# One softmax shift per unit, added as the exponential's bias, in an attention kernel with an FP8 feed-forward

## The chip, the core and the metric

The kernel runs on one core of a Trainium2 chip. A core has five engines that run their own in-order instruction streams: TensorE (PE in the profile, with its weight loads listed apart as PEld), VectorE (DVE), ScalarE (ACT), GpSimd (POOL) and SyncE (SP). DMA transfers are issued by some of these and run beside them. The metric is the device time of one execution in microseconds (us); less is better. Before the change the median of three runs is 1726.01 us (1724.27 to 1728.25).

## The reference

The input x has 2 batches of 2048 rows of 512 values. What has to be computed, cut to its core:

```python
x = x + attention(layernorm(x))              # 16 heads of 32, 2 groups of keys and values
x = x + ffn(layernorm(x))                    # one 512x512 product, both sides rounded to FP8

q, k = rope(xn @ wq + bq) * 32**-0.5, rope(xn @ wk + bk)
scores = q @ k_of_the_group.T * 32**-0.5     # 2048 x 2048 for each head
attn   = softmax(scores)                     # exp(s - m) / sum(exp(s - m)), for any shift m of a row
out    = (attn @ v) @ wo + bo
```

A softmax needs no particular shift: any number m that is the same for a whole row cancels between the exponentials and their sum. The shift only keeps the exponentials in the range of the number format.

## The kernel before, in words

**Units, rounds and chunks.** Attention is done in 64 units. A unit `u` is one block of 512 queries, four heads ("quad") and one half of the block: 4 heads x 256 queries against all 2048 keys. The keys are taken in 16 chunks of 128, four to a round, so a unit has four rounds, `r` = 0 to 3. A chunk's scores stand transposed in PSUM, keys on the 128 partitions and 4 x 256 queries along the row: tile `T`, in one of two buffers, even chunks in one and odd chunks in the other.

**A chunk.** `probabilities` (L1008) has PE multiply the stacked keys `dkS` with the stacked queries `qst` (two matmuls of 512 columns, L1022), and ACT takes the exponential of the 128x1024 scores into `p` (L1031). The score matmuls of chunk c+2 wait until the exponential of chunk c has read the buffer. Keys are stored as differences against the key 256 places earlier, so that chunk c+2 adds to what stands in the buffer (`start=False`); the scores of chunks 0 and 1 open each buffer.

**The shift before.** For each unit the maximum of every row's scores over the first 128 keys is found a unit ahead. `first_scores` (L511) runs in rounds 0 and 1 of the unit before: four matmuls (L523) and a DVE maximum per head and query (L531). `split_maxima` (L500) splits the maxima into two addends in round 2 (L504, L505). `gather_maxima` (L538) transposes them on PE in round 3 (L543) and ACT copies them to `mT` (L547). When the unit starts, four matmuls (L1013) with the constant matrix `sel`, which holds -1, write the negated maxima of all queries into each of the two buffers ahead of the scores. The exponential's bias is a constant.

**Values and sums.** One round later, `weigh` multiplies the `p` of the round with the values (L968, 16 products, `avs`), and the sums of the exponentials are gathered: DVE adds `p` of chunks 0 and 1 to `pair` and of chunks 2 and 3 to a second tile (`add_pair`, L1005); a DMA that GpSimd issues adds `pair` onto the second (`accumulate`, L1035), which leaves one tile `far[r]` a round. DVE joins some of these (`join`, L1038), and PE multiplies what is left with a matrix of ones (`sum_up`, L986), which sums over the partitions. `in_two` says for which units (all but the last three) two tiles are left. Then `keep_values` (L1056) and `finish_heads` (from L935) divide: ACT copies the sums and takes Ln and Exp (L942, L943), DVE does three products (L946 to L948). `seen` collects the sums, so that the end of the program can tell whether some sum was out of range; if so, a slow general version in the same program runs.

**The order of the work.** It is written out by hand: within `manual_schedule` every engine executes its instructions in the order in which the code issues them. In a round the code issues: scores and exponentials of the first two chunks, their sum on DVE, the value products of the round before, `sum_up` of the unit before where due, up to two DVE pieces of other work (`fill(ON_DVE, 2)`), in round 3 a join and `gather_maxima`; then the scores and exponentials of the last two chunks, their sum, `first_scores` in rounds 0 and 1, one or two PE pieces of other work (`fill(ON_PE, ...)`; a piece is one chunk of a projection, two recorded matmuls of 512 columns), and again up to two DVE pieces. The other work is a queue of jobs: projections of queries and keys for later blocks, the output projection, the second layer norm. The job `finish_heads` comes ahead of these.

**Buffers.** `first_scores` and `gather_maxima` use the PSUM bank `s0`, one at a time; the other work uses `s1`. The tiles `far` have four buffers, those of `pair` three, `p` seven.

Of the kernel before, what the change touches and what calls it, by code (L numbers as in the profile page):

```python
# [8 lines left out]
F32 = mybir.dt.float32  # L9
F32R = mybir.dt.float32r  # L10
BF16 = mybir.dt.bfloat16
U32 = mybir.dt.uint32
AF = mybir.ActivationFunctionType
ALU = mybir.AluOpType
AX = mybir.AxisListType

P = 128
HEADS = 16
GROUPS = 2
HD = 32  # L20
TB = 512
NT = TB // P
EPS = 1e-5
E4M3_MAX = 448.0
# [3 lines left out]
def preln_attn_fp8_ffn_kernel(  # L28
# [37 lines left out]
    nc = tc.nc  # L66
# [19 lines left out]
    AV_BANKS = 2  # L86
    FIRST = P
    MOST_BITS = float(0x5D5E0B6B)

    const = ctx.enter_context(tc.tile_pool(name="const", bufs=1))  # L90
    xpool = ctx.enter_context(tc.tile_pool(name="x", bufs=3))
# [90 lines left out]
    ones = const.tile([P, HD], F32, tag="ones", name="ones")  # L182
    nc.gpsimd.memset(ones, 1.0)

    sel = const.tile([P, 4, P], F32R, tag="sel", name="sel")
    nc.gpsimd.memset(sel.bitcast(F32), 0.0)
    for j in range(4):
        nc.gpsimd.memset(sel[j * HD : j * HD + 2, j, :].bitcast(F32), -1.0)
    mrow = const.tile([P, HB], F32R, tag="mrow", name="mrow")
    nc.gpsimd.memset(mrow.bitcast(F32), 0.0)  # L190


    def layernorm_stats(src, mean, rstd, name, tiles=range(NT)):
# [17 lines left out]
    def quantized_scale(amax, scale, inv, name):  # L211

        across = bank(f"across_{name}")
        nc.tensor.transpose(across[:1, :P], amax, ident)
        whole = small.tile([1, 1], F32, tag="whole", name=f"whole_{name}")
        nc.vector.tensor_reduce(whole, across[:1, :P], AX.X, ALU.max)
        give_back()
        down = bank(f"down_{name}")

        nc.tensor.matmul(down[:, :1], sel[:1, 0, :].bitcast(F32), whole, start=True, stop=True)  # L220
        nc.vector.tensor_scalar(scale, down[:, :1], -1.0 / E4M3_MAX, 1e-12, ALU.mult, ALU.max)
        give_back()
        nc.vector.reciprocal(inv, scale)

# [269 lines left out]
    def group(k):  # L494
        return quads[k][1] // (QUADS // GROUPS)

    split = []
    largest = {}

    def split_maxima():  # L500

        if split:
            mview, mx = split.pop()
            nc.vector.tensor_copy(mview[:, :, :, 0], mx)  # L504
            nc.vector.tensor_tensor(  # L505
                mview[:, :, :, 1], mx, mview[:, :, :, 0].bitcast(F32), ALU.subtract
            )

    def first_scores(u, i):

        k, half = units[u]
        if i == 0:
            largest[u] = small.tile([P, HT, 4], F32, tag="mx", name=f"mx_{u}")
        mx = largest[u]
        s = ps_s.tile([P, 4, FIRST], F32, tag="s0", name=f"s_{u}_{i}")  # L520
        at = (half * HT + i) * P
        for j in range(4):
            nc.tensor.matmul(  # L523
                s[:, j, :],
                qst[k][:, j, at : at + P],
                stacked["dkS"][:, group(k), :FIRST],
                start=True,
                stop=True,
                skip_group_check=True,
            )  # L530
        nc.vector.tensor_reduce(mx[:, i, :], s, AX.X, ALU.max)  # L531
        if i == HT - 1:
            mview = mrow.rearrange("p (i j r) -> p i j r", i=HT, j=4)
            split.append((mview, largest.pop(u)))

    maxima = {}

    def gather_maxima(u):  # L538

        split_maxima()  # L540
        tp = ps_s.tile([P, TB], F32, tag="s0", name=f"mtp_{u}")
        for i in range(HT):
            nc.tensor.transpose(  # L543
                tp[:, i * P : (i + 1) * P], mrow[:, i * P : (i + 1) * P].bitcast(F32), ident
            )
        mT = wide.tile([P, HB], F32R, tag="mT", name=f"mT_{u}")
        nc.scalar.copy(mT, tp[:, :HB])  # L547
        maxima[u] = mT


    mean2 = const.tile([P, NBLK, NT], F32, tag="mean2", name="mean2")
# [150 lines left out]
    with tc.manual_schedule():  # L702
        xnT = {
            0: wide_block("xnT", "xnT_kv_0"),
            1: wide_block("attn", "xnT_kv_1", 2),
            2: wide_block("attn", "xnT_kv_2", 2),
            3: wide_block("qst", "xnT_kv_3", 2),
        }
        kv = {n: project_kv(n, x_kv[n], xnT[n], tables[n]) for n in (0, 1)}
        q0 = project_q(0, xnT[0], tables[0])  # L710
        run(first(kv[0], FRONT))
        together((kv[0], 1), (first(kv[1], FRONT), 2))
        x_kv[3] = load_x(3, "kv")
        kv[2] = project_kv(2, x_kv[2], xnT[2], load_tables(2))
        w_all = ppool.tile([P, DC, D], BF16, tag="p", name="w_ffn")
        nc.sync.dma_start(w_all, w_ffn.rearrange("(c p) k -> p c k", p=P))
        queries = first(q0, 1 + QUERIES)
        together((kv[1], 1), (queries, 1), (first(kv[2], FRONT), 2))
        assert (0, 0) in q_far
        stack_queries(0)  # L720
        nc.sync.dma_start(wo_sb, wo.rearrange("(c p) n -> p c n", p=P))
        queries = first(q0, QUERIES)
        together((kv[2], 1), (queries, 1))
        kv[3] = project_kv(3, x_kv[3], xnT[3], load_tables(3))

        run(first(kv[3], FRONT))
        run(prepare_weight(w_all))
        for i in range(HT):
            first_scores(0, i)
        run(first(kv[3], MIDDLE))  # L730
        gather_maxima(0)
        run(kv[3])


# [71 lines left out]
        return 2 if r >= 2 and owed > (ROUNDS + r - 2) * left else 1  # L806

    seen = const.tile([P, len(units)], F32, tag="seen", name="seen")
    without_x = {}
    x_res = {}  # L810
    x_taken, x_done = [], set()
# [122 lines left out]
    def finish_heads(u, both, sums):  # L934
# [4 lines left out]
        nc.scalar.activation(total, sums, AF.Copy, accum_out=seen[:, u : u + 1])  # L939
        yield LATER  # L940
        yield ON_DVE
        nc.scalar.activation(guess, total, AF.Ln)  # L942
        nc.scalar.activation(guess, guess, AF.Exp, scale=-1.0)  # L943
        yield LATER
# [30 lines left out]
                    skip_group_check=True,  # L975
                )

    def in_two(u):

        return 0 <= u < len(units) - 3  # L980

# [26 lines left out]
    def probabilities(u, T, kc):  # L1008

        k, half = units[u]  # L1010
        if kc < 2:
            for j in range(4):
                nc.tensor.matmul(  # L1013
                    T[:, j, :],
                    sel[:, j, :],
                    maxima[u],
                    start=(j % 2 == 0),
                    stop=True,
                    skip_group_check=True,
                )  # L1020
        for j in range(0, 4, 2):
            nc.tensor.matmul(  # L1022
                T[:, j : j + 2, :],
                stacked["dkS"][:, group(k), kc * P : (kc + 1) * P],
                qst[k][:, j : j + 2, half * HB : (half + 1) * HB],
                start=False,
                stop=True,
                skip_group_check=True,
            )
        p = ppool.tile([P, 4, HB], F32, tag="p", name=f"p_{u}_{kc}")  # L1030
        nc.scalar.activation(p, T, AF.Exp, scale=SCALE)  # L1031
        return p

    def accumulate(to, of):
# [2 lines left out]
    def join(to, of):  # L1037
        nc.vector.tensor_tensor(to, to, of, ALU.add)  # L1038
# [19 lines left out]
    with tc.manual_schedule():  # L1058
        behind = None
        before = None  # L1060
        for u, (k, half) in enumerate(units):
# [13 lines left out]
            for r in range(ROUNDS):  # L1075
# [13 lines left out]
                if behind:  # L1089
                    weigh(*behind)  # L1090
                if before and r == 0:
                    parts = before.far[1 : 2 if in_two(before.u) else 3]
                    sum_up(before.avs[:, 1, :], parts, False, False)
                    keep_values(before)
                elif before and r == (2 if in_two(before.u) else 1):
                    sum_up(before.avs[:, 1, :], before.far[3:], False, True)
                    finishing.append(
                        Job(finish_heads(before.u, before.both, before.avs[:, 1, :]))
                    )
                fill(ON_DVE, 2)  # L1100
                if r == 2:
                    split_maxima()
                if last:
                    join(unit.far[1], unit.far[0])
                    if u + 1 < len(units):
                        gather_maxima(u + 1)

                probs.append(probabilities(u, banks[0], chunks[2]))
                probs.append(probabilities(u, banks[1], chunks[3]))
# [1 line left out]
                    unit.far.append(add_pair(u, chunks[2], *probs[2:]))  # L1111
                    accumulate(unit.far[r], pair)
                add_some_bias()
                if before and r == 1 and in_two(before.u):
                    join(before.far[3], before.far[2])
                behind = unit, chunks, probs
                if r < HT and u + 1 < len(units):
                    first_scores(u + 1, r)
                fill(ON_PE, pieces(u, r, ending_soon))
                fill(ON_DVE, 2)  # L1120
            before = unit
# [77 lines left out]
            multiplied(n, i, ready)  # L1199
            ready = ahead  # L1200

    top = small.tile([P, 1], F32, tag="top", name="top")
    nc.vector.tensor_reduce(top, seen.bitcast(U32), AX.X, ALU.max)
    across = bank("across_seen")
    nc.tensor.transpose(across[:1, :P], top, ident)
    flag = small.tile([1, 1], mybir.dt.int32, tag="flag", name="flag")
    nc.vector.tensor_reduce(top[:1], across[:1, :P], AX.X, ALU.max)
    nc.vector.tensor_scalar(flag, top[:1], MOST_BITS, None, ALU.is_gt)
    over = nc.values_load(flag, min_val=0, max_val=1)


# [259 lines left out]
```

## Time and profile before

| what | value |
|---|---|
| median of three runs | 1726.01 us |
| the profiled execution | 1724.88 us, span 1723.0 us |
| granted TensorE clock, mean over the span | 0.975 |
| PE / DVE / ACT / POOL busy | 1575.1 / 1248.8 / 1236.4 / 317.1 us |
| exponentials, L1031 | 1024 of 1024 ns, 992.6 us busy |
| scores, L1022 | 2048 matmuls, 680.0 us busy |
| value products, L968 | 8192 matmuls, 495.1 us busy |
| shift matmuls, L1013 | 512 matmuls, 94.5 us busy |
| sum products, L986 | 1048 matmuls, 80.7 us busy |
| the units run | from 99 to 1608 us of the span |

A line of a group names the kernel's line, the engine, the operation, the tile written and the tiles read, the shapes, the number of instructions, then "busy us, mean ns of one", and at last the time in which the engine stood idle just before them with what ended it. A matmul in float32 is recorded as two instructions. Matmuls overlap each other, so the sum of their lengths is more than the busy time. A line of a timeline begins with the start and the length in us and merges neighbours of a kind. "PEclk" is the share of its full clock that TensorE was granted. The chain is followed back from the last instruction, at each step to what released it.

### The profile page before, as it was taken

Reading aid. Unit: us, or ns where it says so; the run is one execution under the profiler, and the core shown is the slowest. Engines: PE = TensorE matmul, PEld = TensorE weight load, DVE = VectorE, ACT = ScalarE, POOL = GpSimd, SP = SyncE. Lnnn points to the kernel's source line nnn. Section 1 sums busy time; section 2 is a strip of 40 time slices with the busy share of each in tenths; the row PEclk is TensorE's granted clock in tenths of the full one; section 3 lists DMA queues with packets and bytes.
Section 4 is the critical chain, followed back from the end, with each engine's and each line's share of the span. In section 5 each row is a group of like instructions: output and inputs, shape, how many; then the busy total and the mean of one; then the engine's idle time right before and its main releaser. Section 6 shows DMA issues by size and latency. Waiting matters only on the chain.

```text
span 1723.0 us, 33241 instructions
## 1 busy us (share of the span) xinstructions
PE 1575.1 (91%) x13483; PEld 900.6 (52%) x13483; DVE 1248.8 (72%) x1673; ACT 1236.4 (72%) x1629; POOL 317.1 (18%) x381
## 2 busy tenths in 40 slices
PE   5499999999999999999999999999999989999565
PEld 2255555555555555555555555555555555555222
DVE  4447677677887769776877687767777686676697
ACT  2257877777777777777777777877777777777375
POOL 3321112211212112211221122111211122111100
PEclk9699999999999999999999999999999999999888
DMA  6657769867778767878786688656867597576222
GB/s 203 201 122 178 170 146 216 195 127 160 184 178 164 183 153 160 192 147 195 175 196 134 118 199 177 152 117 154 184 149 154 105 203 145 116 187 138 56 86 112
DMA packets 105810, 272.61 MB, mean 158 GB/s; under 512 B 15920, under 2 KB 16560, under 8 KB 102960
## 3 DMA queue, kind: packets, MB, share of 16 engines
q0 software_dynamic: 41328, 142.10, 44.2%
q1 hardware_dynamic: 61904, 126.92, 25.3%
q8 instruction: 108, 1.77, 0.4%
q10 hardware_dynamic: 2416, 1.38, 0.3%
q14 instruction: 54, 0.44, 0.1%
HBM read 87.36 MB, written 40.89 MB: 74 GB/s over the span
## 4 chain that ended last, share of the span: by engine, by line
PE 67%; DVE 10%; DMA 8%; issue 7%; ACT 5%; SPq 2%; POOL 1%; ACTq 0%; DVEq 0%; POOLq 0%
PE avs L968 23%; PE T L1022 23%; PE po L295 5%; ACT p L1031 5%; PE pq L295 4%; PE T L1013 3%; PE avs L986 3%; PE s L523 2%; DMA pa<-pa 2%; DMA qst<-q_far 2%; PE pk L295 2%; PE mtp L543 1%; DVE v L236 1%; DVE pa L1005 1%; DMA sw_q<-q 1%
## 5 line engine op out<-in xcount | busy, mean ns | idle before, releaser
L1031 ACT ACTIVATE p<-T 128x1024 f32<-128x1024 f32 x1024 | 992.6, 1024 | 178.3 <-PE T L1022 171.1
L1005 DVE TENSOR_TENSOR pa<-p,p 128x1024 f32<-128x1024 f32 x511 | 624.7, 1223 | 356.1 <-ACT p L1031 355.0
L1022 PE MATMUL T<-qst,dkS 128*128 128x512 f32 x2048 | 680.0, 442 | 24.8 <-ACT p L1031 23.8
L968 PE MATMUL avs<-p,vX 128*32 128x256 f32 x8192 | 495.1, 382 | 0.0
L1022 PEld LDWEIGHTS T<-qst,dkS 128*128 128x128 f32 x2048 | 338.7, 188 | 273.6 <-ACT p L1031 153.5
L1035 POOL DMA_DIRECT2D pa<-pa x255 | 221.0, 867 | 1201.2 <-DVE pa L1005 915.3
L968 PEld LDWEIGHTS avs<-p,vX 128*32 128x32 f32 x8192 | 239.9, 109 | 225.8 <-issue 93.9
L1038 DVE TENSOR_TENSOR pa<-pa,pa 128x1024 f32<-128x1024 f32 x125 | 152.3, 1219 | 16.0 <-DMA pa<-pa 15.9
L295 PE MATMUL po<-wo_sb,attn 128*128 128x512 f32 x256 | 129.6, 603 | 0.0
L295 PE MATMUL pq<-xnT_q,wq_sb 128*128 128x512 f32 x224 | 111.8, 601 | 0.0
L1013 PE MATMUL T<-mT,sel 128*128 128x256 f32 x512 | 94.5, 307 | 6.5 <-ACT p L1031 6.1
L1013 PEld LDWEIGHTS T<-mT,sel 128*128 128x128 f32 x512 | 72.9, 188 | 46.9 <-ACT p L1031 30.8
L986 PE MATMUL avs<-pa,ones 128*32 128x256 f32 x1048 | 80.7, 382 | 11.9 <-DVE pa L1038 11.1
L531 DVE TENSOR_REDUCE mx<-s 128x4 f32<-128x512 f32 x128 | 87.5, 683 | 2.8 <-PE s L523 2.8
L1056 ACT COPY both<-avs 128x256 f32<-128x256 f32 x64 | 23.9, 373 | 86.7 <-PE avs L986 86.7
L523 PEld LDWEIGHTS s<-dkS,qst 128*128 128x128 f32 x512 | 77.2, 192 | 14.7 <-DVE mx L531 3.1
L939 ACT ACTIVATE both<-avs 128x256 f32<-128x256 f32 x64 | 24.6, 385 | 71.7 <-PE avs L986 71.7
L523 PE MATMUL s<-dkS,qst 128*128 128x128 f32 x512 | 72.8, 265 | 2.2 <-DVE mx L531 2.1
L295 PEld LDWEIGHTS po<-wo_sb,attn 128*128 128x128 f32 x256 | 44.3, 190 | 17.6 <-issue 11.0
L986 PEld LDWEIGHTS avs<-pa,ones 128*32 128x32 f32 x1048 | 27.8, 109 | 43.7 <-DVE pa L1038 30.4
L295 PEld LDWEIGHTS pq<-xnT_q,wq_sb 128*128 128x128 f32 x224 | 39.4, 190 | 17.4 <-issue 13.5
L1171 PE MATMUL xtp<-ident_bf,xq 128*128 128x128 bf16 x128 | 16.0, 266 | 34.3 <-DVE xq L237 34.3
(128 smaller groups left out, 1033.0 us busy)
## 6 DMA issues: line engine op xcount, KB each, us to landing
pa<-pa POOLq DMA_DIRECT2D x255, 512.0 KB, 5.2
qst<-q_far SPq DMA_DIRECT2D x128, 256.0 KB, 7.0
q_far<-hi_q SPq DMA_DIRECT2D x32, 256.0 KB, 4.6
q_far<-lo_q SPq DMA_DIRECT2D x32, 256.0 KB, 4.5
x_res<-in_L_attn_x_dram SPq DMA_DIRECT2D x16, 512.0 KB, 10.8
x_res<-in_L_attn_bo_dram POOLq DMA_DIRECT2D x32, 256.0 KB, 6.7
out_dram<-v SPq DMA_DIRECT2D x16, 512.0 KB, 2.8
sw_q<-q SPq DMA_DIRECT2D x240, 32.0 KB, 3.1
```

What stands on the lines that cost most here:

```text
L295: nc.tensor.matmul(dst, lhs(c), rhs(c), start=(c == 0), stop=(c == chunks - 1))
L523: nc.tensor.matmul(s[:, j, :], qst[k][:, j, at : at + P], stacked["dkS"][:, group(k), :FIRST], start=True, stop=True, skip_group_check=True,)
L531: nc.vector.tensor_reduce(mx[:, i, :], s, AX.X, ALU.max)
L939: nc.scalar.activation(total, sums, AF.Copy, accum_out=seen[:, u : u + 1])
L968: nc.tensor.matmul(av[j * HD : (j + 1) * HD, :], vX[batch(k)][:, kc, group(k), :], p[:, j, :], start=(kc == 0), stop=(kc == NTS - 1), tile ...
L986: nc.tensor.matmul(dst[j * HD : (j + 1) * HD, :], ones, part[:, j, :], start=start and i == 0, stop=stop and i == len(parts) - 1, tile_pos ...
L1005: nc.vector.tensor_tensor(pa, a, b, ALU.add)
L1013: nc.tensor.matmul(T[:, j, :], sel[:, j, :], maxima[u], start=(j % 2 == 0), stop=True, skip_group_check=True,)
L1022: nc.tensor.matmul(T[:, j : j + 2, :], stacked["dkS"][:, group(k), kc * P : (kc + 1) * P], qst[k][:, j : j + 2, half * HB : (half + 1) * H ...
L1031: nc.scalar.activation(p, T, AF.Exp, scale=SCALE)
L1035: nc.gpsimd.dma_start(out=to, in_=of, accum_op=ALU.add)
L1038: nc.vector.tensor_tensor(to, to, of, ALU.add)
```

## The change

Each unit now has a single shift instead of one for every row. The maximum of the scores over the first 128 keys is taken over all heads and queries of the unit, multiplied by -1/32 and handed to the exponential as its bias, a column of 128 equal numbers.

- `first_scores` is one matmul of 512 columns in each of rounds 0 and 1, with keys on the partitions, and a DVE maximum over the row.
- `gather_largest`, at the end of round 2 behind the sum of chunks 2 and 3 and ahead of the PE pieces: DVE takes the larger of the two columns in bf16, PE transposes that column to one row, DVE takes its maximum.
- `spread_largest`, in round 3 behind the sum products: PE multiplies the number with a row of -1/32 in bf16, so that it stands on 128 partitions. `make_shift`, behind the join of round 3: DVE copies it to SBUF.
- The eight matmuls with `sel` at a unit's start are gone, the scores of chunks 0 and 1 open the buffers, and the exponential takes `shift` as bias.
- For all units but the last three, DVE joins `far[1]` and `far[2]` to `far[3]` in rounds 1 and 2 of the next unit, and there is one sum product, in round 3 instead of rounds 0 and 2. The job `finish_heads` starts one round later.
- `finish_heads` also takes the least sum of each unit, and the end of the program tests it too.

```diff
+    scales = const.tile([1, P], BF16, tag="scales", name="scales")
+    nc.gpsimd.memset(scales, -SCALE)
...
     def first_scores(u, i):
...
-        for j in range(4):
-            nc.tensor.matmul(
-                s[:, j, :],
-                qst[k][:, j, at : at + P],
-                stacked["dkS"][:, group(k), :FIRST],
...
-        nc.vector.tensor_reduce(mx[:, i, :], s, AX.X, ALU.max)
...
+        s = ps_s.tile([FIRST, 2, HB], F32, tag="s0", name=f"s_{u}_{i}")
+        nc.tensor.matmul(
+            s,
+            stacked["dkS"][:, group(k), :FIRST],
+            qst[k][:, 2 * i : 2 * i + 2, half * HB : (half + 1) * HB],
...
+        nc.vector.tensor_reduce(
+            largest[u][:, i : i + 1], s.rearrange("p j t -> p (j t)"), AX.X, ALU.max
+        )
+
+    def gather_largest(u):
+
+        mx = largest.pop(u)
+        top = small.tile([P, 1], BF16, tag="top_u", name=f"top_{u}")
+        nc.vector.tensor_tensor(top, mx[:, :1], mx[:, 1:], ALU.max)
+        across = ps_s.tile([P, TB * 2], BF16, tag="s0", name=f"across_{u}")
+        nc.tensor.transpose(across[:1, :P], top, ident_bf)
+        largest[u] = small.tile([1, 1], BF16, tag="whole_u", name=f"whole_{u}")
+        nc.vector.tensor_reduce(largest[u], across[:1, :P], AX.X, ALU.max)
+
+    def spread_largest(u):
+
+        down = ps_s.tile([P, TB], F32, tag="s0", name=f"down_{u}")
+        nc.tensor.matmul(down[:, :1], scales, largest.pop(u), start=True, stop=True)
+        shift[u] = down
+
+    def make_shift(u):
+
+        down = shift[u]
+        shift[u] = small.tile([P, 1], F32, tag="shift_u", name=f"shift_{u}")
+        nc.vector.tensor_copy(shift[u], down[:, :1])
...
         nc.scalar.activation(total, sums, AF.Copy, accum_out=seen[:, u : u + 1])
         yield LATER
         yield ON_DVE
+        nc.vector.tensor_reduce(least[:, u : u + 1], total, AX.X, ALU.min)
         nc.scalar.activation(guess, total, AF.Ln)
...
     def probabilities(u, T, kc):
...
-        if kc < 2:
-            for j in range(4):
-                nc.tensor.matmul(
-                    T[:, j, :],
-                    sel[:, j, :],
-                    maxima[u],
...
-                start=False,
+                start=kc < 2,
...
-        nc.scalar.activation(p, T, AF.Exp, scale=SCALE)
+        nc.scalar.activation(p, T, AF.Exp, bias=shift[u], scale=SCALE)
...
                 if before and r == 0:
-                    parts = before.far[1 : 2 if in_two(before.u) else 3]
-                    sum_up(before.avs[:, 1, :], parts, False, False)
+                    if not in_one(before.u):
+                        sum_up(before.avs[:, 1, :], before.far[1:3], False, False)
                     keep_values(before)
-                elif before and r == (2 if in_two(before.u) else 1):
+                elif before and r == (3 if in_one(before.u) else 1):
                     sum_up(before.avs[:, 1, :], before.far[3:], False, True)
...
+                if last and u + 1 < len(units):
+                    spread_largest(u + 1)
                 fill(ON_DVE, 2)
-                if r == 2:
-                    split_maxima()
                 if last:
                     join(unit.far[1], unit.far[0])
-                    if u + 1 < len(units):
-                        gather_maxima(u + 1)
+                elif before and r > 0 and in_one(before.u):
+                    join(before.far[3], before.far[r])
+                if last and u + 1 < len(units):
+                    make_shift(u + 1)
...
                 add_some_bias()
-                if before and r == 1 and in_two(before.u):
-                    join(before.far[3], before.far[2])
                 behind = unit, chunks, probs
-                if r < HT and u + 1 < len(units):
+                if r < 2 and u + 1 < len(units):
                     first_scores(u + 1, r)
+                if r == 2 and u + 1 < len(units):
+                    gather_largest(u + 1)
                 fill(ON_PE, pieces(u, r, ending_soon))
                 fill(ON_DVE, 2)
```

Ahead of the first unit the same calls take the place of `first_scores` and `gather_maxima`. At the end of the program DVE reduces `seen` and `least`, tests both against their bounds and takes the larger verdict, instead of reducing and testing `seen` alone.

## The prediction

> **What bounds the kernel now.** I read the page's shares first, then its chain, the groups, one unit in the timeline, and last the clock.
>
> ```profile
> span 1723.0 us, 33241 instructions
> PE 1575.1 (91%) x13483; PEld 900.6 (52%) x13483; DVE 1248.8 (72%) x1673; ACT 1236.4 (72%) x1629; POOL 317.1 (18%) x381
> PE 67%; DVE 10%; DMA 8%; issue 7%; ACT 5%; SPq 2%; POOL 1%; ACTq 0%; DVEq 0%; POOLq 0%
> L1013 PE MATMUL T<-mT,sel 128*128 128x256 f32 x512 | 94.5, 307 | 6.5 <-ACT p L1031 6.1
> L986 PE MATMUL avs<-pa,ones 128*32 128x256 f32 x1048 | 80.7, 382 | 11.9 <-DVE pa L1038 11.1
> ```
>
> PE is busy 91% of the time and holds 67% of the chain. The last two lines are most of what the change takes from PE: 94.5 us and half of 80.7 us. If PE were the only limit, that would be a gain of some 130 us. So I ask of each round whether PE really ends it. Here are rounds 2 and 3 of one unit, first PE, then ACT and DVE (start, length):
>
> ```profile
> 965.43 1.62 PE L1022 MATMUL T<-qst,dkS 128*128 128x512 f32 x4
> 966.98 1.93 PE L968 MATMUL avs<-p,vX 128*32 128x256 f32 x32
> 968.73 0.62 PE L986 MATMUL avs<-pa,ones 128*32 128x256 f32 x8
> 969.28 1.19 PE L1022 MATMUL T<-qst,dkS 128*128 128x512 f32 x4
> 970.31 1.02 PE L295 MATMUL po<-wo_sb,attn 128*128 128x512 f32 x2
> 971.18 0.73 PE L1022 MATMUL T<-qst,dkS 128*128 128x512 f32 x2
> 972.10 0.73 PE L1022 MATMUL T<-qst,dkS 128*128 128x512 f32 x2 [0.18 <-ACT p L1031]
> ...
> 970.10 3.85 ACT L1031 ACTIVATE p<-T 128x1024 f32<-128x1024 f32 x4 [0.21 <-PE T L1022]
> ...
> 972.08 1.23 DVE L1005 TENSOR_TENSOR pa<-p,p 128x1024 f32<-128x1024 f32 x1 [1.40 <-ACT p L1031]
> ```
>
> Call a round's four chunks c0 to c3. PE issues c2 and c3 at 969.28, their exponentials run from 970.10, the second ends at 972.05, and only then do two things start: DVE's sum of both (972.08), and PE's scores for c1 of the next round (972.10), which need c3's bank. So a round is a loop of PE and ACT. Cutting the same timeline finer gives its links: from c1's first score matmul to c2's second one 2.81 us, from there to c2's exponential 0.49, two exponentials 1.94 (they start 0.92 apart and the last takes 1.02), and 0.06 to the next c1: 5.30 us, which is round 1 (961.02 to 966.32). One piece of projection (0.86 us) fits beside ACT; with two pieces (1.72) PE ends the loop instead. Units with one piece per round last 22.8 us, those with two in rounds 2 and 3 last 23.9.
>
> **The change part by part.** I follow c1's first score matmul from round to round, in the one-piece unit: before, 5.66 (r=0), 5.30 (r=1), 5.78 (r=2), 6.07 (r=3).
>
> *Exponential with a bias tile.* The bias was a constant, now it is a column in SBUF. The nearest rows have the same size, with and without such a column:
>
> ```profile
> L439 ACT ACTIVATE q<-pq,bq_sb 128x512 f32<-128x512 f32 x32 | 22.1, 689 | 3.7 <-PE pq L295 3.7
> L285 ACT COPY xnT_kv<-tp_kv 128x512 f32<-128x512 f32 x32 | 18.9, 590 | 20.8 <-PE tp_kv L282 20.8
> ```
>
> That is 99 ns more each; the start of the next instruction comes 0.10 later too (585 against 482 ns), so overlap doesn't hide it. I take 0.095 us for each of 1024 exponentials. In the loop a pair costs 2.13 instead of 1.94. Ends: 0 (hidden) to 0.10.
>
> *Shift matmuls (L1013), 8 a unit.* Four stood ahead of c0 and four ahead of c1 in round 0, 0.12 us apart, 0.95 in all. In a one-piece unit the first four lie in PE's wait for c3's bank; the other 0.48 are saved. With two pieces all 0.95 are.
>
> *First scores.* 4 matmuls (0.41 us) become one of 512 columns (0.23), in rounds 0 and 1. Both lie between c3's scores and the wait for c3's exponential: worth nothing, because ACT ends that stretch. If that cover went, 0.18 twice.
>
> *Sum products.* Two groups of 0.54 us become one, moved to r=3. They stand between c1 and c2, on the loop: r=0 and r=2 save 0.54 each, r=3 pays 0.54.
>
> *Transposes and the copy mT.* Two transposes at r=3 (0.37 us) go; the matmul that spreads the maximum comes in the same place. Its nearest row, the spread of a scale at L220, takes 0.24 alone; I take 0.2, ends 0.05 and 0.36. The copy (0.27 of ACT) was in ACT's wait for c2, so nothing.
>
> *The new transpose at r=2: the decisive item.* It stands on PE right behind c3's scores, ahead of the projection piece and the whole next round. It needs the maximum over two columns, which DVE does behind its sum of c2 and c3 in its in-order queue; that sum waits for c3's exponential. In the unit shown: c3's exponential would end at 972.05+0.19 = 972.24, the sum starts 0.03 later, the next instruction on DVE 1.14 after that (so follow the sums), 973.41; a small one takes 0.17, 973.58; a release of PE by DVE takes 0.07 (L1038's end at 968.66 to 968.73); loading one column 0.08 (L214). The transpose runs at 973.73 and the piece follows at 973.85 instead of 970.31: 3.54 later. Then 0.86 and 0.46 (c0) to c1 at 975.17 instead of 972.10, 3.07 later, less 0.49 because the sums no longer delay c2: +2.6. PE had had its last score matmul at 970.08, 0.40 long, so it idles 3.2 us. A transpose itself lies between 0.05 and 0.37 (L214), taken at 0.12.
>
> *DVE.* Per unit: third join +1.14, least value +0.35 (half of the 128x512 reduction's 0.68), two halves of the old split -0.35, three small ones +0.5: +1.7 on about 17.7 of 23.6 us. Between the sums of c2 and c3 in rounds 1 and 2 it then does two sums 2.3, one join 1.14, one reduction 0.6: 4.0 of 5.5 us, leaving 1.5 for filler. I take no delay; the cover goes where two or more fillers of 0.6 come. The reduction of one row waits about 0.4 for the transpose with only filler behind it; the copy of the shift waits for the spread with the sum of c2 and c3 behind it, which isn't ready by then. The exponential that uses the shift is 6 us later. The joins moved past nothing on SP or POOL; no DMA is added.
>
> *The heads' end, one round later.* Ln and Exp move on ACT from r=3 to r=0, where the value copy is. From 958.35 before; without the sums it would start at about 0.2 ahead of c2's second score matmul (2.6 after c1), then 0.27, 0.45 and 0.35: c2's exponential can start at 3.7, not 3.3. So r=0 becomes 3.7+2.13+0.06 = 5.89 (before 5.66): +0.23, although PE lost 1.2 us of work there.
>
> *Sum of a unit.* r=0 +0.23; r=1 5.49, +0.19; r=2 +2.6; r=3: 2.81+0.54+0.2+0.49+2.13+0.06 = 6.23, +0.16: +3.2. With two pieces: +0.23, +0.19, +3.1 (the second piece is no longer hidden in ACT's wait), and r=3 PE-bound 6.42 for 6.76, -0.34: again +3.2. Of the 64 units 63 have the new transpose: +202. PE's waits for joins ahead of the sums (11.9 us in the row above) mostly go: -10. Before and behind the units a few small instructions, +1.5.
>
> *The clock.* Does a 3.2 us hole cost TensorE its clock? The clock in the records changes on a grid of 3.41 us. Windows of that grid (length, PE busy, clock):
>
> ```profile
> core 0: us, PE busy (x), PEclk, DMA share, GB/s
> 1647.18:1650.59 3.41, 1.60 (x11) 1.00 0.21 82
> 1650.59:1654.00 3.41, 1.26 (x9) 1.00 0.41 156
> 1654.00:1657.41 3.41, 2.78 (x13) 0.50 0.21 80
> ```
>
> After 1.81 us idle in a window the clock stays; after 2.15 it is 0.50 for the whole next one. Another window with 1.90 idle (1616.46) lost it too. So the limit is near 1.85. A hole of 3.2 us, put anywhere on the grid, leaves 1.85 in one window in about 87% of positions. The next window then has 2.8 to 3.4 us of PE work at half speed: matmuls of 0.43 took 0.85 in such a window (90.70). If only scores and projections slow, 1.0 us a unit on average; if the value products do too, 1.3. I take 1.16 x 63 = 73; ends 0 and 85.
>
> The Trainium skill weighs this otherwise. Its page "TensorE: Matmul & The Clock Gate" (section "Why this matters for your kernels") asks for no idle gap over about 3 us and names one whole window of idle as the condition; by its 3.4 us window this hole would just keep the clock, and the sum would be 1918. The trace's 1.90 and 2.15 us decide for me.
>
> The profiled execution took 1724.88 us (1723.0 span and 1.9 around it), 1.1 below the median of 1726.01, which is nothing here. 1724.9 + 202 - 10 + 1.5 + 73 = 1991.
>
> **The rivals.**
> - *The clock holds.* For it: in the stretch of the units the clock never fell, even with a hole of 2.4 us; against it: that hole was split over two windows, 1.00 and 1.43. Then 1918.
> - *DVE becomes late.* One filler more ahead of the maximum in every unit: 0.6 x 63 = +38, 2029; two, 2067. For it: 1.5 us of slack only; against it: 0.68 to 1.9 us of idle before most of its sums.
> - *Not slower: the maximum is there in time.* If the transpose found it ready, r=2 would be 5.49 for 5.78, and a one-piece unit would come out even (+0.23+0.19-0.29+0.16 = +0.3, less the waits); a two-piece one -0.2. About 1715, and 1675 if the bias column were free as well. It decides only if PE waits less than about 0.25 us a unit, where I work out 3.2; the order of the two DVE instructions in the code is against it.
>
> **How the numbers follow.** Stall and clock 0.52, the clock holds 0.25, DVE late 0.14, in time 0.04; 0.05 for a stall half covered by something not seen. The range goes from below the second case (1918 with a free bias column, 0.76 x 35 one-piece units = -27) to the third: 1890 to 2060. Differences below 0.2% (3.5 us) can't be told from none: faster 0.04, same 0.02, slower 0.94.
>
> **What would show it.** PE idle 3.2 us before the new transpose, released by DVE's small maximum, 63 times; exponentials of 1.12 us; L1005 and then the maximum at c3's end in round 2; half-clock windows right behind, the granted clock of the run falling from 0.975 to about 0.92; units of 27 us. I am wrong if the transpose comes without a wait, or if the exponentials stay at 1.02.

## The result and the profile after

The changed kernel takes 2059.99 us, median of four runs (2055.94 to 2060.61), against 1726.38 before. The ratio is 1.193 (95% interval 1.191 to 1.195): 19% slower, 334 us. The forecast was 1991 with a range of 1890 to 2060, so the sign and the main reason hold. That the time lies inside the range at all is luck: it is 0.01 us from the edge, and two of the four runs are beyond it. The 69 us more than forecast need a cause of their own.

The page of the changed kernel, its shares, chain, and the groups that answer to those of before, with the new transpose:

```profile
span 2057.9 us, 30646 instructions
PE 1624.0 (79%) x12094; PEld 836.6 (41%) x12099; DVE 1351.9 (66%) x1865; ACT 1291.2 (63%) x1565; POOL 315.6 (15%) x377
PE 38%; DVE 28%; ACT 15%; issue 8%; DMA 5%; SPq 3%; POOL 1%; ACTq 0%; DVEq 0%; POOLq 0%
L1018 ACT ACTIVATE p<-T,shift 128x1024 f32<-128x1024 f32 x1024 | 1070.9, 1112 | 446.2 <-PE T L1009 432.6
L527 PE MATMUL across<-ident_bf,top 128*1 128x128 bf16 x64 | 15.8, 247 | 252.1 <-DVE top L525 252.1
```

PE went from 91% to 79% busy, and no engine took its place: DVE and ACT are less busy in share too. The chain says why: PE's part fell from 67% to 38%, DVE's rose from 10% to 28% and ACT's from 5% to 15%. The engines now wait for each other in turn. The last line names the place: PE stood idle for 252.1 us ahead of 64 small transposes, released by DVE's small maximum `top`; the matmuls themselves take 15.8 us. That is 4.00 us for each of the 63 waits. Exponentials take 1112 ns for 1024.

One unit in the timeline of the changed kernel, round 2 and the start of round 3; PE, then ACT and DVE:

```profile
1199.38 1.21 PE L1009 MATMUL T<-qst,dkS 128*128 128x512 f32 x4
1203.73 0.22 PE L527 MATMUL across<-ident_bf,top 128*1 128x128 bf16 x1 [3.13 <-DVE top L525]
1203.87 1.77 PE L294 MATMUL po<-wo_sb,attn 128*128 128x512 f32 x2
1204.65 2.70 PE L1009 MATMUL T<-qst,dkS 128*128 128x512 f32 x4
...
1200.22 2.12 ACT L1018 ACTIVATE p<-T,shift 128x1024 f32<-128x1024 f32 x2 [1.41 <-PE T L1009]
...
1202.37 1.22 DVE L1002 TENSOR_TENSOR pa<-p,p 128x1024 f32<-128x1024 f32 x1 [0.60 <-ACT p L1018]
1203.52 0.15 DVE L525 TENSOR_TENSOR top<-mx 128x1 bf16<-128x1 f32 x1
```

Read it from 1200.22: two exponentials end at 1202.34, DVE's sum starts 0.03 later, `top` follows at 1203.52, the transpose at 1203.73. PE had been idle for 3.13 us by then. The projection behind the transpose takes 1.77 us where it took 1.02 before, and four score matmuls 2.70 instead of 1.20, because of the clock. The two windows of the clock's grid (length, PE busy, clock) that hold this stretch:

```profile
core 0: us, PE busy (x), PEclk, DMA share, GB/s
1200.81:1204.22 3.41, 0.50 (x2) 1.00 0.52 98
1204.22:1207.64 3.41, 3.41 (x10) 0.50 0.52 101
```

With 2.91 us idle in the first, the second ran at half speed. In the stretch of the units the records hold 300 us at half clock, 88 windows of 3.41; before there were none. The granted clock of the whole run fell from 0.975 to 0.906.

### The profile page after: what moved, and what is told of

Its sections match the earlier page's. It is cut to its first block, busy times and chain, and to the rows that moved or that the text cites. A ratio compares the mean times of both kernels' runs of the same rounds, so it can differ in the third digit from the quotient of the medians.

```text
span 2057.9 us, 30646 instructions
## 1 busy us (share of the span) xinstructions
PE 1624.0 (79%) x12094; PEld 836.6 (41%) x12099; DVE 1351.9 (66%) x1865; ACT 1291.2 (63%) x1565; POOL 315.6 (15%) x377
## 4 chain that ended last, share of the span: by engine, by line
PE 38%; DVE 28%; ACT 15%; issue 8%; DMA 5%; SPq 3%; POOL 1%; ACTq 0%; DVEq 0%; POOLq 0%
PE avs L965 14%; PE T L1009 12%; ACT p L1018 12%; DVE pa L1002 11%; DVE pa L1025 5%; PE po L294 4%; PE pq L294 4%; DMA pa<-pa 3%; SPq L307 2%; DVE mx L517 2%; PE avs L983 1%; PE pk L294 1%; DVE v L235 1%; DMA qst<-q_far 1%; ACT both L940 1%
## 5 line engine op out<-in xcount | busy, mean ns | idle before, releaser
L1018 ACT ACTIVATE p<-T,shift 128x1024 f32<-128x1024 f32 x1024 | 1070.9, 1112 | 446.2 <-PE T L1009 432.6
L1009 PE MATMUL T<-qst,dkS 128*128 128x512 f32 x2048 | 736.8, 471 | 77.7 <-ACT p L1018 75.3
L1009 PEld LDWEIGHTS T<-qst,dkS 128*128 128x128 f32 x2048 | 367.6, 201 | 425.9 <-ACT p L1018 275.3
L965 PE MATMUL avs<-p,vX 128*32 128x256 f32 x8192 | 519.9, 396 | 0.0
L1025 DVE TENSOR_TENSOR pa<-pa,pa 128x1024 f32<-128x1024 f32 x186 | 226.3, 1216 | 9.2 <-DMA pa<-pa 9.2
L527 PE MATMUL across<-ident_bf,top 128*1 128x128 bf16 x64 | 15.8, 247 | 252.1 <-DVE top L525 252.1
L294 PE MATMUL pq<-xnT_q,wq_sb 128*128 128x512 f32 x224 | 135.3, 713 | 0.0
L517 DVE TENSOR_REDUCE mx<-s 128x1 f32<-128x512 f32 x128 | 87.4, 683 | 2.1 <-PE s L510 2.1
L510 PE MATMUL s<-qst,dkS 128*128 128x512 f32 x128 | 51.8, 405 | 0.8 <-DVE mx L517 0.8
L281 PE MATMUL tp_kv<-ident,xn_kv 128*128 128x128 f32 x128 | 23.6, 328 | 27.2 <-DVE xn_kv L262 26.6
L294 PE MATMUL pk<-xnT_kv,wkv_sb 128*128 128x512 f32 x64 | 39.3, 727 | 7.4 <-ACT xnT_kv L284 7.4
```

Source lines behind the costliest of these rows:

```text
L281: nc.tensor.transpose(tp[:, c * P : (c + 1) * P], xn[h][:, c * P : (c + 1) * P], ident)
L294: nc.tensor.matmul(dst, lhs(c), rhs(c), start=(c == 0), stop=(c == chunks - 1))
L510: nc.tensor.matmul(s, stacked["dkS"][:, group(k), :FIRST], qst[k][:, 2 * i : 2 * i + 2, half * HB : (half + 1) * HB], start=True, stop=True,)
L517: nc.vector.tensor_reduce(largest[u][:, i : i + 1], s.rearrange("p j t -> p (j t)"), AX.X, ALU.max)
L965: nc.tensor.matmul(av[j * HD : (j + 1) * HD, :], vX[batch(k)][:, kc, group(k), :], p[:, j, :], start=(kc == 0), stop=(kc == NTS - 1), tile ...
L1009: nc.tensor.matmul(T[:, j : j + 2, :], stacked["dkS"][:, group(k), kc * P : (kc + 1) * P], qst[k][:, j : j + 2, half * HB : (half + 1) * H ...
```

## The experiments

Every kernel was timed beside the kernel before on the same chip; ratios are to that. "After" is the changed kernel.

### The place of the stall, its clock, DVE's lateness and the bias column

**top_early**: DVE takes the larger column a round earlier, so that the transpose finds it ready.

```diff
+    def larger_column(u):
+
+        mx = largest.pop(u)
+        largest[u] = small.tile([P, 1], BF16, tag="top_u", name=f"top_{u}")
+        nc.vector.tensor_tensor(largest[u], mx[:, :1], mx[:, 1:], ALU.max)
+
     def gather_largest(u):
 
-        mx = largest.pop(u)
-        top = small.tile([P, 1], BF16, tag="top_u", name=f"top_{u}")
-        nc.vector.tensor_tensor(top, mx[:, :1], mx[:, 1:], ALU.max)
+        top = largest.pop(u)
...
                     first_scores(u + 1, r)
+                if r == 1 and u + 1 < len(units):
+                    larger_column(u + 1)
```

> One edit to the changed kernel: DVE takes the larger of the two columns at the end of round 1, right behind the maximum of the second first scores, instead of at the end of round 2 behind the sum of chunks 2 and 3; the transpose on PE stays where it is. Theory 'stall' (PE waits at the transpose because DVE reaches the maximum only behind that sum): the wait of 252 us before the transpose goes, the clock stays at 1.00 through the units, and the time is what the bias column and the heads' end leave of the savings, 1690 to 1730 us. Rival 'ACT' (the loss is the longer exponentials and the later Ln and Exp on ACT, and the wait at the transpose only shows time that ACT would take anyway): over 1900 us. In between, 1740 to 1890: both.

Measured: 1776.02 us, ratio 1.029 (1.025 to 1.032). One small instruction moved in DVE's queue gives back 284 of the 334 us. The wait before the transpose falls from 252 us to 15.6. So the stall at that place is shown, and the rival "ACT" (over 1900) is out. But the time is above the 1690 to 1730 that the theory asked for. One-piece units come out as worked out in the prediction's third rival, nearly even: 22.92 us against 22.81. The 50 us that are left sit in 19 units, which are over 1 us longer than before. Here is the end of one such unit, DVE and then ACT of top_early:

```profile
764.90 0.75 DVE L312 SCALAR_TENSOR_TENSOR sw_q<-sw_q,sign,cs 128x512 f32<-128x512 f32 x1 [7.03 <-DMA sw_q<-q]
765.57 0.68 DVE L328 TENSOR_TENSOR q<-q,cs 128x512 f32<-128x512 f32 x1
766.29 0.69 DVE L329 TENSOR_TENSOR q<-sw_q,q 128x512 f32<-128x512 f32 x1
766.90 1.22 DVE L1030 TENSOR_TENSOR pa<-pa,pa 128x1024 f32<-128x1024 f32 x1
768.03 0.15 DVE L545 COPY shift<-down 128x1 f32<-128x1 f32 x1
...
768.30 1.11 ACT L1023 ACTIVATE p<-T,shift 128x1024 f32<-128x1024 f32 x1 [7.47 <-DVE shift L545]
```

A filler on DVE (a piece of the other work) waits 7.03 us for a DMA. The copy of the next unit's shift, 0.15 us of work, stands behind it and behind a join, and the next unit's first exponential waits 7.47 us for that copy. It is the same mistake at a second place: in the whole run ACT waits 43.0 us for that copy, in 20 waits.

**filled_hole**: dead matmuls keep TensorE busy in the hole.

```diff
+        if u > 0:
+            dead = ps_s.tile([P, TB], F32, tag="s0", name=f"dead_{u}")
+            for _ in range(14):
+                nc.tensor.matmul(dead, ident_bf, wT[:, 0, :], start=True, stop=True)
         across = ps_s.tile([P, TB * 2], BF16, tag="s0", name=f"across_{u}")
```

> The changed kernel with 14 matmuls of 512 columns in bf16 ahead of each unit's transpose (not of the first unit's), into the bank that the transpose uses next; their result is not read. They take some 3.0 us, so they lie in the hole in which PE waits for the maximum, and only keep TensorE busy. Theory 'clock' (the hole costs TensorE its clock behind it): granted clock in the units near 1.00, and about 1.3 us for each of the 88 half-clock windows come back, 115 us: 1945 us (1920 to 1985). Rival 'no price' (the half clock falls where ACT or DVE end the stretch): 2050 to 2075 us.

Measured: 1957.68 us, ratio 1.134 (1.130 to 1.137), 102 us less than after, with 14 more matmuls in each unit. The granted clock of the run is 0.970. All 63 transposes still wait for `top`, most of them 0.1 us, so the dead matmuls hold none of them up. So the lost clock costs at least 102 us, and "no price" is out. The units show the two parts apart, too. The one-piece units that follow each other undisturbed (36, 37, 43 to 45) last 22.81 us before (unit 43: 23.1), 25.75 with the hole filled, and 27.30 after: 2.94 us of the new order with the clock kept, and 1.55 of clock.

**joins_early**: the two joins for the unit before, one round earlier.

```diff
-                elif before and r > 0 and in_one(before.u):
-                    join(before.far[3], before.far[r])
+                elif before and r < 2 and in_one(before.u):
+                    join(before.far[r + 2], before.far[r + 1])
```

> One edit to the changed kernel: DVE's joins for the unit before come one round earlier, in rounds 0 and 1 instead of 1 and 2 (far[1] to far[2], then far[2] to far[3]); their number and the sum product in round 3 stay. Theory 'DVE late' (of the mean wait of 4.0 us before the transpose 0.8 us come from DVE being late at the sum of chunks 2 and 3, and the join of round 2 is 1.14 us of that work): the mean wait falls to 3.2 to 3.5 us, and with the second half-clock windows that go the time falls by 35 to 80 us, to 1980 to 2025 us. Rival 'other work' (the lateness comes from the other DVE pieces, wherever the joins stand): 2050 to 2070 us.

Measured: 2013.70 us, ratio 1.165 (1.162 to 1.169), 46 us less than after; the mean wait before the transpose is 3.37 us instead of 4.00. That is theory "DVE late". What the lateness looks like in the changed kernel, DVE, PE and ACT in a unit with two fillers:

```profile
1314.45 1.22 DVE L1025 TENSOR_TENSOR pa<-pa,pa 128x1024 f32<-128x1024 f32 x1
1315.77 1.23 DVE L1002 TENSOR_TENSOR pa<-p,p 128x1024 f32<-128x1024 f32 x1
1316.91 0.68 DVE L517 TENSOR_REDUCE mx<-s 128x1 f32<-128x512 f32 x1
1317.51 1.21 DVE L1002 TENSOR_TENSOR pa<-p,p 128x1024 f32<-128x1024 f32 x1
1318.65 0.68 DVE L247 TENSOR_TENSOR lo_q<-q,hi_q 128x512 fp32r<-128x512 f32 x1
1319.25 1.22 DVE L1025 TENSOR_TENSOR pa<-pa,pa 128x1024 f32<-128x1024 f32 x1
1320.57 1.23 DVE L1002 TENSOR_TENSOR pa<-p,p 128x1024 f32<-128x1024 f32 x1
...
1321.92 0.27 PE L527 MATMUL across<-ident_bf,top 128*1 128x128 bf16 x1 [4.69 <-DVE top L525]
...
1316.86 2.12 ACT L1018 ACTIVATE p<-T,shift 128x1024 f32<-128x1024 f32 x2 [0.89 <-PE T L1009]
```

DVE has no gap here: two joins, three sums, a maximum and a piece of a filler follow each other, and the sum that `top` stands behind starts at 1320.57 although its exponentials had ended at 1318.98. PE's wait is 4.69 us, where it is 3.13 when DVE is not late. The expected 3.2 to 3.5 us of wait and 1980 to 2025 us both hold.

**before_column**: the kernel before with a column of zeros as bias.

```diff
-        nc.scalar.activation(p, T, AF.Exp, scale=SCALE)
+        nc.scalar.activation(p, T, AF.Exp, bias=zero, scale=SCALE)
```

> The kernel before with one edit: the exponential gets a column of zeros in SBUF as its bias instead of the constant. Exponentials of 1.12 us instead of 1.02. By the sum of the prediction it costs 0.76 us in each of about 35 units with one piece per round and 0.38 in the others: +37 us, 1763 us (1750 to 1775). If PE hides it: 1726. If every exponential's 0.095 us lands on the path: 1823.

Measured: 1757.00 us, ratio 1.018 (1.014 to 1.022), +31 us. Exponentials take 1114 ns for 1024, 92 us in all, and a third of that reaches the path. One-piece units last 23.51 us, +0.70 where the sum had 0.76.

### What is left when the transpose doesn't wait

**before_one**: the kernel before with the changed sums alone.

```diff
-                    parts = before.far[1 : 2 if in_two(before.u) else 3]
-                    sum_up(before.avs[:, 1, :], parts, False, False)
+                    if not in_one(before.u):
+                        sum_up(before.avs[:, 1, :], before.far[1:3], False, False)
                     keep_values(before)
-                elif before and r == (2 if in_two(before.u) else 1):
+                elif before and r == (3 if in_one(before.u) else 1):
...
+                elif before and r > 0 and in_one(before.u):
+                    join(before.far[3], before.far[r])
...
-                if before and r == 1 and in_two(before.u):
-                    join(before.far[3], before.far[2])
```

> The kernel before with the changed kernel's sums alone: the third join on DVE, one sum product per unit in round 3, the heads' end one round later; shift, maxima and the constant bias as before. By the steps of the prediction with the constant bias: round 0 +0.04 us (Ln and Exp come ahead of c2's exponential), round 2 -0.49 to -0.54, round 3 +0.54, so nothing, less the waits for joins of 12 us, plus DVE where it is late at the joins: 1715 to 1735 us. If PE were the only limit: half of the sum products, 63 x 0.54 = 34 us, 1692.

Measured: 1747.52 us, ratio 1.009 (1.008 to 1.011): half of the sum products off PE, and the kernel is slower. One-piece units last 22.78 us against 22.81, so the steps were right there: nothing. What I missed is in a few units: unit 5 lasts 29.5 us (24.0 before), unit 27 29.5 (24.5), unit 62 30.3 (25.0). From the waits of before_one:

```profile
DVE sw_q L313 <- DMA sw_q<-q: 36.6, 12, 8.5
```

Before, that line was 7.0 us in 5 waits. A filler that meets a DMA that has not landed holds all of DVE. This goes with the changed sums in every run without the long stall: DVE waits 21.5 to 36.6 us at that line in the five kernels that have them (before_one, top_early, both_early, shift_by_act, row_shift) and 2.0 to 7.0 us in the four that have the old ones (before, before_column, act_two, row_two). My reading is that the heads' end, a round later, moves the fillers into other slots; no run separates it from the third join. In unit 62 it is PE that waits, 5.26 us at the sum products, released by the DMA that adds `pair`.

**both_early**: after with both early edits.

> The changed kernel with both edits: the larger column at the end of round 1, and the joins in rounds 0 and 1. Theory 'two DVE waits' (what top_early has left over the kernel before, 50 us, is 31 us of the bias column and the rest units that wait for DVE, whose shift copy stands behind the joins and fillers of rounds 2 and 3): fewer late units, 1745 to 1770 us. Rival (the rest is the heads' end on ACT, which neither edit moves): 1770 to 1780 us.

Measured: 1777.85 us, ratio 1.027 (1.025 to 1.029): no different from top_early alone. Theory "two DVE waits" fails in the form in which I put it: fewer joins ahead do not help once the transpose no longer waits for them. ACT still waits 44.6 us for the shift's copy in 19 waits, and DVE's fillers still wait 24.8 us for their DMA (21.5 in top_early), which neither edit moves. The rival's number is met, its reason isn't shown by this run.

**shift_by_act**: top_early, and the shift's copy taken off DVE; ACT makes it behind chunk 3's exponential of round 3.

```diff
-        nc.vector.tensor_copy(shift[u], down[:, :1])
+        nc.scalar.copy(shift[u], down[:, :1])
...
-                if last and u + 1 < len(units):
-                    spread_largest(u + 1)
...
-                if last and u + 1 < len(units):
-                    make_shift(u + 1)
...
+                if last and u + 1 < len(units):
+                    spread_largest(u + 1)
+                    make_shift(u + 1)
```

> The changed kernel with the larger column at the end of round 1, and the spread moved to the end of round 3 (behind c3's scores, ahead of the PE pieces) with ACT instead of DVE copying the shift to SBUF behind c3's exponential. The joins stay in rounds 1 and 2. Theory 'two DVE waits': ACT's waits for DVE's shift copy (43 us in 20 waits in top_early) and PE's for the row's maximum ahead of the spread go, and about 0.2 us of ACT come in each unit: 1735 to 1755 us, which is near the kernel before with a bias column, 1757. Rival (those waits only lie over others, DMA above all): 1765 to 1780 us.

Measured: 1756.09 us, ratio 1.015 (1.013 to 1.017), 20 us less than top_early by the medians, a little above the expected 1735 to 1755 and far from the rival. So the second DVE wait is real too. What stays is the bias column and the sums.

**row_shift**: both early edits, no bias column; DVE makes a row of 512 shifts and four matmuls of one row write it into the score buffers.

```diff
+        shift[u] = small.tile([1, TB], BF16, tag="shift_u", name=f"shift_{u}", bufs=2)
+        nc.vector.tensor_scalar(shift[u], minus, whole, None, ALU.mult)
...
+                nc.tensor.matmul(
+                    T[:, j : j + 2, :].rearrange("p j t -> p (j t)"),
+                    scales,
+                    shift[u],
...
-        nc.scalar.activation(p, T, AF.Exp, bias=shift[u], scale=SCALE)
+        nc.scalar.activation(p, T, AF.Exp, scale=SCALE)
```

> The changed kernel with both early edits and without the bias column: DVE multiplies a row of 512 times -1 with the unit's maximum right behind that maximum, and four matmuls of one row (0.22 us each) write the shift into the two score buffers when the unit starts, so the exponential's bias is a constant again. The spread and the copy of the shift go. By the steps: round 0 5.70 us, rounds 1 and 2 5.30, round 3 6.27, 22.6 for 22.8 in a one-piece unit, some 0.3 less in the others, and no unit waits for a copy on DVE: 1700 to 1725 us, less than the kernel before. Rival (DVE is still late with the row in units with many fillers): 1730 to 1750 us.

Measured: 1771.39 us, ratio 1.024 (1.022 to 1.026), no better than the column and worse than shift_by_act. The expectation fails, and by more than the rival's number. One-piece units last 22.99 us and not 22.6. Counted as in the expectation, from c1's first score matmul, rounds 0 to 3 take 5.68, 5.29, 5.35 and 6.67: the first three are near what was expected, round 3 is 0.40 longer. From the end of that round in unit 36, PE and then ACT:

```profile
1014.61 0.60 PE L1005 MATMUL T<-shift,scales 1*128 1x512 bf16 x2
1015.14 0.73 PE L1014 MATMUL T<-qst,dkS 128*128 128x512 f32 x2
1015.81 0.60 PE L1005 MATMUL T<-shift,scales 1*128 1x512 bf16 x2
...
1013.46 1.94 ACT L1023 ACTIVATE p<-T 128x1024 f32<-128x1024 f32 x2 [0.22 <-PE T L1014]
```

The second exponential ends at 1015.40 and frees c1's bank, but PE, which has no gap here, comes to c1's shift only at 1015.81. With the sums, a projection piece and the row matmuls behind each other, PE ends this round, where the expectation let ACT end it. Most of the other excess is in long units (18 are over 1 us longer than before, 37 us together); DVE waits 28.9 us for `sw_q` there.

**act_two** and **row_two**: shift_by_act and row_shift with the sums of the kernel before (two joins, two products, the heads' end a round earlier).

> shift_by_act with the sums of the kernel before: two joins, two sum products in rounds 0 and 2, the heads' end a round earlier. What is left of the change is the single shift with its bias column. Theory 'parts add' (the changed sums cost some 17 us by themselves, as on the kernel before, because fillers and joins on DVE then meet DMAs that have not landed): 1735 to 1745 us, about 10 to 15 us over the kernel before, since the column's 31 us come against the shift matmuls and transposes that are gone. Rival (the changed sums cost nothing beside the new shift): 1752 to 1760 us.

> row_shift with the sums of the kernel before: no bias column, the shift written by four matmuls of one row, two joins, two sum products. Theory 'parts add': 17 us less than row_shift, 1750 to 1758 us. If the joins and the heads' end are what makes DVE late with the row in the units with many fillers, more: 1715 to 1735 us, as the kernel before or a little less. Rival (the row on DVE and its matmuls are what costs): 1765 to 1775 us.

Measured: act_two 1727.68 us, ratio 1.000 (0.998 to 1.001); row_two 1753.00 us, ratio 1.014 (1.011 to 1.016). So one shift per unit as the exponential's bias, without the waits and with the old sums, is worth nothing either way: the column's 31 us and what the shift matmuls, first scores and transposes gave back cancel. In the one-piece units rounds 0 to 2 are longer by 0.24, 0.18 and 0.18 us and round 3 is shorter by 0.59. The changed sums cost more in act_two's company (28 us by the medians) than alone (17); in row_two it is 18, so "parts add" holds there and is short for act_two. No kernel of the study beats the kernel before beyond its interval.

## Why the prediction was right or wrong

Taken apart by ratios, each times 1726 us, the 334 us are: 102 the clock (after to filled_hole), 182 the wait at the transpose with the clock kept (filled_hole to top_early), 23 the shift's copy on DVE (to shift_by_act), 27 the sums (to act_two), and nothing for the shift itself. The first two shares are exact only as far as the dead matmuls restore the clock: 24 us at half clock were left in the units. Against the forecast that is 29 us more of clock (102 for 73) and 40 more of the rest (232 for 192).

- *What bounds the kernel.* Right. A round is a loop of PE and ACT; half of the sum products off PE gave nothing in the one-piece units (before_one), and 8 shift matmuls, 6 of the 8 first-score matmuls and the transposes gave back 31 us (before_column to act_two), nearly all of it in round 3, which fell from 6.22 to 5.48 us there. If PE were the only limit, they would have been worth over 94.
- *The new transpose.* Right in place and size. Forecast: 3.2 us of idle, released by `top`, 63 times; the trace has 3.13 us in the undisturbed units. A one-piece unit with the clock kept was to be 3.2 us longer; it is 2.94. By rounds that is +0.21, +0.18, +2.66 and -0.11, where the forecast had +0.23, +0.19, +2.6 and +0.16.
- *DVE: "I take no delay".* Wrong, and the step that failed. I had the slack, 1.5 us between the sums for fillers, and let it stand for the average unit. But fillers come in bunches: in 29 of the 63 units the sum ahead of `top` starts more than 0.1 us late, by 0.3 to 4.1 us. The mean wait is 4.00 us, so this term measures 0.87 x 63 = 55 us of waiting where I had 0; joins_early gets 46 of time back. The other terms without the clock together came out 15 lower than forecast, which leaves the 40. The rival "DVE becomes late" had the size right (2029 to 2067) and got 0.14 of the chance. It was not a rival but an addition, and its number fits in part by luck: it held no more clock, and 29 of the 69 us are clock.
- *The clock.* Right in mechanism, too small in size: 73 forecast, 102 measured, above the 85 that I gave as its end. The price of a window was right (102 us for the 81 or so that went, 277 us of the 300 at 3.41 each, 1.26 a window; I had 1.0 to 1.3). The number was not: 0.87 a unit forecast, 88/63 = 1.4 measured. The 34 undisturbed waits are followed by 34 slow windows, the 27 waits of 4.48 us or more by 49. So most of it follows from the failed step on DVE. The value products slowed too (634 instead of 379 ns in such windows), which I had left open.
- *The Trainium skill's rule.* "TensorE: Matmul & The Clock Gate" (section "Why this matters for your kernels") asks for no idle gap over about 3 us and makes an idle whole window the condition. The hole of 3.13 us is over the first figure and under the 3.41 of a window, so the two disagree about it, and the prediction weighed only the second. The trace differs from the second: in the changed kernel all 59 full-speed windows with 1.90 us or more idle lost the clock for the next one, and none up to 1.87 did. In other runs the limit is not that sharp (1.91 kept it in filled_hole, 1.66 lost it in top_early, 1.43 in before_one). The measurement decides: about half of a window is enough.
- *The bias column.* Right. 31 us by itself on the kernel before (37 worked out), 1114 ns an exponential there and 1112 after.
- *The sums and the heads' end.* Right for a quiet unit (nothing), wrong for the whole: +17 us alone, +27 in the end. DVE's fillers meet late DMAs in just the runs that have these sums; what in the new order brings that about is not shown. I had counted -10 there.
- *The rival "in time".* It asked for 1715 and top_early measured 1776: I had looked at one of the two places where PE or ACT hangs on DVE's queue. The shift's copy I costed at nothing, with "6 us later" as its cover; a filler's wait of 7 us is longer than that cover. The copy is 23 of the 50 us that top_early has over the kernel before, the sums 27.

## What to carry to other kernels

A value that one engine needs early must not be made behind an engine's longest wait: ask for each new instruction what stands ahead of it in its own in-order queue, and what that waits for, before asking what it costs. An instruction of 0.15 us, queued behind one sum of 1.2 us that waits for ACT, cost a kernel 284 us here. The stall on TensorE was paid twice, once as time (182 us) and once as clock (102). And slack of an engine that also does bunched filler work is to be read in the worst unit, not the mean one.

## What the runs showed of the hardware that I had not expected

A window of the clock's grid with 1.9 us or more of its 3.41 idle lost the clock for the next one (one with 1.91 in filled_hole kept it), and a window at half clock cost 1.26 us on average.

Undisturbed units of the changed kernel last 27.30 to 27.32 us, eight windows of 3.413, where two units that happened to keep the clock (55 and 57) last 24.88 and 25.73. It looks as if the loop fell into step with the clock's grid, but that is not shown. The transposes of units 35 to 37 start 2.91 to 2.93 us into a window and those of units 43 to 45 1.90 to 1.92, with the same length of unit, and 25.75 and one price of 1.55 make 27.30 too.

A matmul that reads one row of a 1x512 operand takes as long as one that reads 128: in row_shift the 256 matmuls with a single row have a mean length of 379 ns, as much as the dead bf16 matmuls of filled_hole on all 128 rows (379), and they start 0.23 us apart where those start 0.22. But the clock seems not to count it as much work. In row_shift and row_two five windows with only 0.64 to 0.70 us idle lost the clock. Each holds four of these matmuls; with their time counted as idle, the five have 1.62 to 1.68 (two more of such windows, with 1.60 and 1.64, kept it). The 53 windows of these two kernels that hold none of them and have 0.6 to 1.5 us idle all kept it. No run tests this by itself.
